# A two-layer attention and Fourier kernel: the transform along h taken apart into even and odd frequencies

## Chip, cores and metric

The kernel runs on one core of a Trainium2 chip. The metric is the device time of one execution in microseconds; the time before is a median of three runs. Arithmetic is in 32-bit floats throughout, except for two small bf16 mask tables.

## The reference

The input x is 8 images of 128 x 128 pixels with 64 channels (axes b, h, w, c). Two layers follow each other.

```
# layer 0: criss-cross attention, for every pixel along its column and its row
Q, K = x @ w_q, x @ w_k          # 8 channels each
V = x @ w_v                      # 64 channels
energy_H = Q . K along h, own pixel set to -inf
energy_W = Q . K along w
att = softmax over the 128 + 128 energies
x = gamma * (att_H V + att_W V) + x

# layer 1: a Fourier mixer, then a depthwise MLP
h  = layernorm(x) @ w_te                     # 128 channels
F  = fft2(h) over h and w
fc = gelu([re F, im F] @ w_fc)
x1 = x + real(ifft2(fc_re + i fc_im)) @ w_tp
h2 = layernorm(x1) @ w_fe                    # 128 channels
d  = gelu(3x3 depthwise convolution of h2)
out = x1 + d @ w_fp
```

The discrete transform is done with matrix products. A transform of 128 lines along h can be split: with s = line n + line n+64 and d = line n - line n+64, the even frequencies are a transform of the 64 lines of s, the odd ones of the 64 lines of d.

## The kernel before

The kernel has two stages that follow each other.

**attention()** goes over 64 tasks: for each image four H blocks and then four W blocks of 32 columns or lines. Step n of its loop turns and projects block n+1, computes the energies of n+1 and n in one pass, and finishes the products of n-1. The order of instructions on each engine is that of the loop's text. For W blocks a tail follows in later steps: `weigh` (n-1, ACT), `total` (n-1, POOL), `invert` (n-2, DVE), `combine` (n-2, POOL: the weighted sum of H and W parts onto x, and the store to x2), and the layer norm, `norm_step`, called four times in a step as parts 0 to 3. Parts 0 and 2 square half a block on ACT (L559) and sum x on DVE (L560), parts 1 and 3 sum the squares (L562), all for block n-4. Part 3 also takes the inverse root for block n-5 on POOL, and for every second W block packs two normed blocks, 64 lines, into the buffer `yw` (L574) and sends them to DRAM as one half of `xn` (L578). `yw` has two buffers, each holding the attention output of two W blocks and then the packed lines; the ACT copies of L409 fill it. In the first W pair of an image it is one buffer, in the second pair the other. For the last three blocks DVE does what POOL does else, and SP the stores.

**mixer()** does the rest. A planner, `Plan.run`, orders the work: every piece has an engine, a cost, a due time, what it follows, and the buffers ("slots") that it takes and frees. The planner is greedy: on each engine the ready piece with the earliest due time goes first. Due times come from the constants of the head (PERIOD, GROUP0, GROUP and so on), so the transforms of image b+1 and the MLP of image b are woven together. For one image the transforms are: `along_w` (PE, all 128 lines of 64 channels to 64 frequencies along w, real and imaginary), `along_h` on 17 groups of up to four frequencies, `keep_h` (ACT, PSUM to SBUF), `channels` (PE), `bend` (ACT, gelu), `hermite` (POOL), `project` (PE), `keep_g` (ACT), then `inverse_h`, `inverse_w` and `add` (DVE). The MLP: `turn`, `expand`, nine taps of the convolution (`first_tap` on ACT, most of the rest on DVE at L1144, some as ACT products that DMAs add, L1138), `bend`, `shrink`, `add` (L1211).

In the mixer PSUM has two slots "fc" of two banks and four slots "mm" of one bank. `along_w`, `along_h`, `project`, `inverse_h`, `inverse_w`, `turn`, `expand` (two at once) and `shrink` share the four. In `along_h` each frequency costs four products of 128 lines by 128 frequencies:

```
nc.tensor.matmul(fps[0:64, n, :], lhsT=re, rhs=cos, start=True, stop=False)
nc.tensor.matmul(fps[64:128, n, :], lhsT=im_, rhs=cos, start=True, stop=False)
nc.tensor.matmul(fps[0:64, n, :], lhsT=im_, rhs=sin, start=False, stop=True)
nc.tensor.matmul(fps[64:128, n, :], lhsT=re, rhs=nsin, start=False, stop=True)
```

A 32-bit product stands in the profile as two instructions.

Of the kernel before, what the change touches and what calls it, by code (L numbers as in the profile page):

```python
# [22 lines left out]
F32 = mybir.dt.float32  # L23
# [3 lines left out]
ALU = mybir.AluOpType  # L27
# [4 lines left out]
P = 128  # L32
C = 64
D8 = 8
HID = 128
R = 32
# [7 lines left out]
BY_DMA, BY_DMA_LAST = (1, 2), 1  # L44


PERIOD, GROUP0, GROUP, BACK0, BACK = 262.0, -1.9, 10.3, 174.8, 4.3
CHUNK0, CHUNK, STAY, LOADX = 18.2, 14.2, 0.1, -10.2
CH = 8
LN = 16  # L50

# [1 line left out]
def dft_tables():  # L53

    n = np.arange(P)
    kw = np.arange(64)
    ang = 2.0 * np.pi * (np.outer(n, kw) % P) / P
    rw = np.stack([np.cos(ang), -np.sin(ang)], axis=2)
    rw[:, 0, 1] = np.where(n % 2 == 0, 1.0, -1.0)
    rw = rw.reshape(P, P)  # L60
    full = 2.0 * np.pi * (np.outer(n, n) % P) / P
    cos, sin = np.cos(full), np.sin(full)
    k = np.arange(64)
    back = 2.0 * np.pi * (np.outer(k, n) % P) / P
    re = 2.0 * np.cos(back) / P
    re[0] = 1.0 / P
    im = -2.0 * np.sin(back) / P
    im[0] = np.where(n % 2 == 0, 1.0, -1.0) / P
    idw = np.concatenate([re, im], axis=0)
    out = np.concatenate([rw, cos, sin, -sin, cos / P, sin / P, -sin / P, idw], axis=1)  # L70
    return np.ascontiguousarray(out.astype(np.float32))


TBL_W = 8 * P


def border_marks():
# [164 lines left out]
def attention(tc, nc, x, w_q, b_q, w_k, b_k, w_v, b_v, gamma, x2, xn, prm, marks, packed):  # L242
    NB = x.shape[0]
    with ExitStack() as ctx:
# [202 lines left out]
        state = {}  # L447
# [27 lines left out]
        def maximum(n):  # L475

            b, way, blk = tasks[n]
            s, o = state[n], img[b]
            cols = slice(blk * R, blk * R + R)
            if way == "H":  # L480
                nc.vector.tensor_copy(o.mh[:, cols].rearrange("p (q i) -> p q i", q=4), s.mneg)
                return
            t = s.t = late.tile([P, 5, R], F32, tag="tsm", name="tsm", bufs=4)
            nc.gpsimd.tensor_tensor(
                t[:, 0, :].rearrange("p (q i) -> p q i", q=4),
                o.mdt[:, 0, cols].rearrange("p (q i) -> p q i", q=4), s.mneg, ALU.subtract,
            )
# [20 lines left out]
        def is_w(n):  # L508
            return 0 <= n < len(tasks) and tasks[n][1] == "W"
# [20 lines left out]
        def combine(n):  # L530
# [13 lines left out]
                    merger(n).tensor_tensor(xv, xv, part, ALU.add)  # L544
            store(n).dma_start(out=x2[b][:, blk * R : blk * R + R, :], in_=s.xb)

        def norm_step(n, part):


            m = n - 4  # L550
            if is_w(m):
                s = state[m]
                h = slice(16 * (part // 2), 16 * (part // 2) + 16)
                sq = s.y[:, h, 0:C]
                if part % 2 == 0:
                    if m >= N - 3:
                        nc.vector.tensor_tensor(sq, s.xb[:, h, :], s.xb[:, h, :], ALU.mult)
                    else:
                        nc.scalar.activation(sq, s.xb[:, h, :], AF.Square)  # L559
                    nc.vector.tensor_reduce(s.t[:, 0, h], s.xb[:, h, :], AX.X, ALU.add)  # L560
                else:
                    nc.vector.tensor_reduce(s.t[:, 1, h], sq, AX.X, ALU.add)  # L562
            m = n - 5
            if is_w(m):
                b, way, blk = tasks[m]
                s = state[m]
                r, q, t = (s.t[:, i, :] for i in range(3))
                if part == 3:
                    inverse_root(merger(m), m >= N - 3, r, q, t)
                if part == 3 and blk % 2 == 1:  # L570
                    z = s.yw.rearrange("p r c -> p (r c)")[:, 0 : 2 * R * C].rearrange("p (c r) -> p c r", c=C)
                    for o, lo in ((state[m - 1], 0), (s, R)):
                        for h in range(0, R, 8):
                            merger(m).tensor_tensor(  # L574
                                z[:, :, lo + h : lo + h + 8].rearrange("p c r -> p r c"), o.xb[:, h : h + 8, :],
                                o.t[:, 0, h : h + 8].unsqueeze(2).to_broadcast([P, 8, C]), ALU.mult,
                            )
                    (nc.sync if m >= N - 3 else nc.gpsimd).dma_start(out=xn[b][:, blk // 2, :, :], in_=z)  # L578

        def across(o, c0):  # L580

# [14 lines left out]
        N = len(tasks)  # L596
        E = mybir.EngineType
        with tc.manual_schedule(engines={E.PE, E.Activation, E.DVE, E.Pool}):
            for n in range(-1, N + 6):
# [18 lines left out]
                    moved(ps.tile([P, 2, 512], F32, tag="ps", name="mt"))  # L618
                if new is not None:
                    new.queries()  # L620
                norm_step(n, 0)
                if last is not None:
                    last.attend(1, 0, last.y)
                    across_all(n - 1)
# [2 lines left out]
                if new is not None:  # L627
                    new.values(0)
                flush(1)
                norm_step(n, 1)  # L630
                if is_w(n - 2):
                    invert(n - 2)
                if new is not None or old is not None:
                    for k in range(2):
                        energies(0, k, new, old, masked)
                norm_step(n, 2)
                if is_w(n - 1):
                    weigh(n - 1)
                if new is not None:
                    new.values(1)  # L640
                if old is not None:
                    target(n)
                    old.attend(0, 1, old.y)
                    old.attend(0, 0, old.y)
                flush(1)
                if new is not None or old is not None:
                    for k in range(2):
                        energies(1, k, new, old, masked)
                if is_w(n - 1):
                    total(n - 1)  # L650
                norm_step(n, 3)
# [8 lines left out]
def mixer(tc, nc, x2, xn, tbl, packed, spread, out):  # L660
    NB = out.shape[0]
    with ExitStack() as ctx:
# [6 lines left out]

        tb = const.tile([P, TBL_W], F32, tag="tb", name="tb")  # L670
        nc.sync.dma_start(out=tb, in_=tbl)
        rw, cos, sin, nsin, cosn, sinn, nsinn, idw = (tb[:, P * i : P * i + P] for i in range(8))
        pk = const.tile([P, PACKED], F32, tag="pk", name="pk")
        nc.sync.dma_start(out=pk, in_=packed[:, 0:PACKED])
        c = fields(pk, PARTS)
# [102 lines left out]
        class Image:  # L778
# [27 lines left out]
                    self.at = big([P, P, C], "at")  # L806
                nc.scalar.copy(self.at[:, :, c0 : c0 + 4], aps.rearrange("p c k -> p k c"))

            def along_h(self, g):

                at = self.at.rearrange("p (k t) c -> p k t c", t=2)
                fps = ps_m.tile([P, 4, P], F32, tag="mm", name="fps")
                for n, k in enumerate(g):
                    if k % 64 == 0:
                        a = at[:, 0, k // 64, :]
                        nc.tensor.matmul(fps[0:64, n, :], lhsT=a, rhs=cos, start=True, stop=True)
                        nc.tensor.matmul(fps[64:128, n, :], lhsT=a, rhs=nsin, start=True, stop=True)
                        continue
                    re, im_ = at[:, k, 0, :], at[:, k, 1, :]
                    nc.tensor.matmul(fps[0:64, n, :], lhsT=re, rhs=cos, start=True, stop=False)  # L820
                    nc.tensor.matmul(fps[64:128, n, :], lhsT=im_, rhs=cos, start=True, stop=False)
                    nc.tensor.matmul(fps[0:64, n, :], lhsT=im_, rhs=sin, start=False, stop=True)
                    nc.tensor.matmul(fps[64:128, n, :], lhsT=re, rhs=nsin, start=False, stop=True)
                return fps

            def keep_h(self, g, fps):
                f = pf.tile([P, 4, P], F32, tag="f", name="f", bufs=3)
                nc.scalar.copy(f[:, 0 : len(g), :], fps[:, 0 : len(g), :])  # L828
                return f

            def channels(self, g, f, half):
# [27 lines left out]
            def project(self, g, gr, gi):  # L859
# [3 lines left out]
                if g[0] == 0:  # L863

                    parts = (
                        (0, gr, 0, wtp, True, False), (0, gi, P, wtpn, False, False), (0, None, 0, btp, False, True),
                        (1, gi, 0, wtp, True, False), (1, gr, P, wtp, False, True),
                    )
                    for t, src, o, w, first, last in parts:
                        for z, zo in halves:  # L870
                            a = e0[:, z] if src is None else src[:, o + zo : o + zo + 64]
                            nc.tensor.matmul(gps[z, 0, t, :], lhsT=a, rhs=w, start=first, stop=last)
                    return gps
                for j in range(len(g)):
                    for t, src in enumerate((gr, gi)):
                        for z, zo in halves:
                            o = j * P + zo
                            nc.tensor.matmul(  # L878
                                gps[z, j, t, :], lhsT=src[:, o : o + 64], rhs=wtp, start=True, stop=True
                            )  # L880
# [65 lines left out]
        def transforms(b):  # L946
# [25 lines left out]
            for i, g in enumerate(GROUPS):  # L972
                n = len(g)
                t = t0 + GROUP0 + GROUP * i
                s, fs, hold = Slot("mm"), Slot("f"), {}
                p = plan.add(
                    "PE", 0.47 * n if i else 0.5, lambda g=g, hold=hold: hold.update(ps=im.along_h(g)), keeps, t, "C", (s,)
                )
                im.last_h.append(p)
                f = plan.add(  # L980
                    "ACT", 0.1 + 0.12 * n, lambda g=g, hold=hold: hold.update(f=im.keep_h(g, hold["ps"])), [p], t + 1,
                    takes=(fs,), frees=(s,),
                )
                sums, outs, p = [], [], None
                for half in range(2):
# [390 lines left out]
```

## Time and profile before

| what | value |
|---|---|
| median of three runs | 3202.73 us (3199.78 to 3213.37) |
| profiled execution | 3198.24 us |
| its span, first to last instruction | 3196.4 us |
| PE busy | 2915.1 us, 91% |
| DVE busy | 2486.9 us, 78% |
| ACT busy | 2096.0 us, 66% |
| POOL busy | 1636.0 us, 51% |
| L1144, taps on DVE | 840 of 1517 ns |
| L838, products of `channels` | 1088 of 598 ns |
| L828 and like copies of 128x512 on ACT | about 0.59 us each |
| L578, xn from POOL | 14 of 2048 KB, 9.4 us to landing |
| L545, x2 from POOL | 30 of 1024 KB, 4.9 us to landing |

Attention takes the first 1275 us or so, the mixer the rest. A row of the page gives line, engine, operation, tiles, shapes and count, then busy time and the mean of one in ns, then how long the engine had been idle before these instructions and which engine and line ended most of that wait. "issue" is a wait that the profile doesn't explain. Busy shares are means over stages with different limits.

### The profile page before, as it was taken

The numbers are of one execution on the slowest core, as the hardware profiler recorded it, in microseconds if no ns is written. First come the engines' busy times: TensorE is split into PE (matmuls) and PEld (weight loads), VectorE is DVE, ScalarE is ACT, GpSimd is POOL, SyncE is SP. The second block draws the span as 40 slices with busy tenths as digits, with TensorE's granted clock in tenths as the row PEclk, the third lists the DMA queues.
The fourth block names the chain that finished last, engine by engine and source line by source line (L and its number), as shares of the span: only waits on it lengthen the run. The fifth ranks groups of instructions, "written<-read, shape, count | busy, mean of one in ns | idle before, by whom it ended". The sixth has DMA issues, their size and how long they took to land.

```text
span 3196.4 us, 110388 instructions
## 1 busy us (share of the span) xinstructions
PE 2915.1 (91%) x50476; PEld 2144.6 (67%) x50476; DVE 2486.9 (78%) x2313; ACT 2096.0 (66%) x2744; POOL 1636.0 (51%) x1974
## 2 busy tenths in 40 slices
PE   7998898988888986999999999999999999999978
PEld 5877777777777776766666575675675675665644
DVE  4575747574747576819999999999999999999996
ACT  3665656565656654537868867767777777777754
POOL 1095959595959585424525516515525425435421
PEclk8999999999999998999999999999999999999989
DMA  6024242424243422242674664655745745745645
GB/s 175 23 96 121 96 130 99 121 95 121 101 132 104 122 95 104 99 159 50 134 172 89 157 144 85 170 117 93 182 105 108 176 96 111 178 94 100 120 90 100
DMA packets 227069, 372.71 MB, mean 117 GB/s; under 512 B 143401, under 2 KB 176812, under 8 KB 208044
## 3 DMA queue, kind: packets, MB, share of 16 engines
q0 software_dynamic: 37072, 188.39, 26.1%
q1 hardware_dynamic: 188764, 177.19, 19.7%
q8 instruction: 396, 6.49, 0.8%
q14 instruction: 69, 0.57, 0.1%
q10 hardware_dynamic: 768, 0.07, 0.0%
HBM read 170.96 MB, written 102.26 MB: 85 GB/s over the span
## 4 chain that ended last, share of the span: by engine, by line
PE 49%; DVE 29%; POOL 9%; issue 6%; DMA 4%; ACT 2%; SPq 0%; POOLq 0%; ACTq 0%; DVEq 0%
DVE acc L1144 16%; PE fcps L838 6%; PE yp L403 6%; PE e L433 4%; PE dps L906 4%; POOL xb L544 3%; PE yps L893 3%; PE yps L895 3%; DVE m L438 3%; PE vps L381 3%; PE tp L348 3%; DMA acc<-pr 3%; PE pq L362 3%; PE op L1206 3%; PE tpy L584 2%
## 5 line engine op out<-in xcount | busy, mean ns | idle before, releaser
L1144 DVE SCALAR_TENSOR_TENSOR acc<-h,pk,acc 128x1024 f32<-128x1024 f32 x840 | 1270.0, 1517 | 49.6 <-ACT acc L1130 28.1
L854 POOL TENSOR_TENSOR gs<-gl 128x512 f32<-128x512 f32 (+2 forms) x272 | 441.9, 1644 | 303.3 <-ACT gl L848 301.9
L838 PE MATMUL fcps<-f,pk 128*128 128x512 f32 (+2 forms) x1088 | 508.9, 598 | 0.2 <-ACT f L828 0.2
L438 DVE TENSOR_REDUCE m<-e 128x8 f32<-128x1024 f32 x256 | 300.6, 1211 | 211.5 <-PE e L433 211.3
L444 ACT ACTIVATE att<-e 128x1024 f32<-128x1024 f32 x256 | 259.7, 1024 | 170.2 <-PE e L433 166.3
L848 ACT ACTIVATE gl<-fcps,pk 128x1024 f32<-128x1024 f32 (+2 forms) x272 | 289.9, 1073 | 96.3 <-PE fcps L838 77.6
L1039 POOL TENSOR_TENSOR xc<-x,st 128x512 f32<-128x512 f32 x128 | 184.1, 1454 | 293.8 <-PE tpn L1073 117.1
L1138 POOL DMA_DIRECT2D acc<-pr x120 | 105.6, 880 | 443.4 <-DVE acc L1144 268.6
L403 PEld LDWEIGHTS yp<-v,att 128*64 128x64 f32 x8192 | 268.9, 143 | 87.3 <-issue 39.6
L433 PE MATMUL e<-kt,qt 32*128 32x128 f32 x4096 | 302.7, 291 | 25.4 <-DVE v L384 13.6
L838 PEld LDWEIGHTS fcps<-f,pk 128*128 128x128 f32 x1088 | 191.9, 193 | 196.2 <-issue 146.4
L403 PE MATMUL yp<-v,att 128*64 128x65 f32 x8192 | 296.8, 229 | 18.9 <-issue 17.3
L433 PE MATMUL e<-qt,kt 32*128 32x128 f32 x4096 | 300.1, 288 | 12.2 <-issue 10.1
L433 PEld LDWEIGHTS e<-kt,qt 32*128 32x128 f32 x4096 | 262.6, 194 | 38.1 <-DVE v L384 17.6
L433 PEld LDWEIGHTS e<-qt,kt 32*128 32x128 f32 x4096 | 258.6, 193 | 19.7 <-issue 13.1
L820 PE MATMUL fps<-tb,at 128*64 128x128 f32 x1008 | 200.4, 281 | 23.3 <-DVE ot L1211 23.3
L1134 ACT ACTIVATE pr<-h,pk 128x1024 f32<-128x1024 f32 x176 | 214.3, 1237 | 0.0
L878 PEld LDWEIGHTS gps<-pk,gs 128*64 128x64 f32 x4032 | 137.3, 144 | 108.7 <-issue 57.5
L1115 ACT ACTIVATE h<-hp,pk 128x512 f32<-128x512 f32 x254 | 156.4, 669 | 71.4 <-PE hp L1095 71.2
L384 DVE TENSOR_TENSOR v<-vps,bv 128x1024 f32<-128x1024 f32 x128 | 156.0, 1218 | 60.6 <-PE vps L381 60.6
L893 PE MATMUL yps<-tb,gt 128*64 128x128 f32 x1024 | 202.0, 279 | 0.6 <-ACT gt L887 0.6
L894 PE MATMUL yps<-tb,gt 128*64 128x128 f32 x1024 | 202.0, 279 | 0.0
(218 smaller groups left out, 7419.9 us busy)
## 6 DMA issues: line engine op xcount, KB each, us to landing
acc<-pr POOLq DMA_DIRECT2D x120, 512.0 KB, 5.4
xb<-in_x_dram SPq DMA_DIRECT2D x32, 1024.0 KB
xn<-xn SPq DMA_DIRECT2D x32, 1024.0 KB
x<-x SPq DMA_DIRECT2D x32, 1024.0 KB
x<-spread POOLq DMA_DIRECT2D x32, 1024.0 KB, 8.4
x<-xb POOLq DMA_DIRECT2D x30, 1024.0 KB, 4.9
out_dram<-ot SPq DMA_DIRECT2D x120, 256.0 KB
xn<-yw POOLq DMA_DIRECT2D x14, 2048.0 KB, 9.4
```

What stands on the lines that cost most here:

```text
L403: nc.tensor.matmul(yq[z, q, j, :], lhsT=att[:, q, j, z], rhs=self.v[:, r, :], start=True, stop=True)
L433: nc.tensor.matmul(e[:, q, j, :], lhsT=left[rows, 4 * a + j, :], rhs=right[rows, 4 * a + j, :], start=not msk, stop=j == 3 or not msk,)
L438: nc.vector.tensor_reduce(new.mneg[:, 2 * k : 2 * k + 2, 4 * a : 4 * a + 4], e1, AX.X, ALU.max, negate=True,)
L444: nc.scalar.activation(att, e2, AF.Exp)
L820: nc.tensor.matmul(fps[0:64, n, :], lhsT=re, rhs=cos, start=True, stop=False)
L838: nc.tensor.matmul(ps[:, sgn, 0:n], lhsT=w[:, cols], rhs=fv, start=True, stop=not mean)
L848: nc.scalar.activation(gl[:, :, 0:n], ps[:, :, 0:n], AF.Gelu, bias=bfc[:, half : half + 1])
L854: nc.gpsimd.tensor_tensor(gs[:, 0:n], gl[:, 0, 0:n], gl[:, 1, 0:n], ALU.add if half == 0 else ALU.subtract)
L893: nc.tensor.matmul(yps[0:64, c, :], lhsT=gr, rhs=cosn, start=True, stop=False)
L894: nc.tensor.matmul(yps[64:128, c, :], lhsT=gi, rhs=cosn, start=True, stop=False)
L1134: nc.scalar.activation(pr, self.lines(k, t), AF.Identity, bias=zero, scale=wdw[:, t : t + 1])
L1144: nc.vector.scalar_tensor_tensor(out=a, in0=self.lines(k, t), scalar=wdw[:, t : t + 1], in1=a, op0=ALU.mult, op1=ALU.add)
```

## The change

Attention no longer stores the first and the last 64 normed lines of an image, but their sum (slot 0 of `xn`) and their difference (slot 1). The first pair of blocks is written to both slots by one DMA with a broadcast source. The second pair is then added to slot 0 by two accumulating DMAs of half the channels each, and subtracted from slot 1: one step later ACT makes negated copies `zn` of 16 channels, and four accumulating DMAs add them. For the last image DVE makes sum and difference, and SP stores both. Parts 0, 1 and 2 of `norm_step` move to later places of the step, and the copy of an H block's maximum moves from DVE to ACT.

In the mixer `along_w` gets sums in its first 64 rows and differences in the last 64. `along_h` treats two groups in one piece of work: each frequency takes eight products of 64 rows by 64 frequencies, on the four quadrants of the array, into two PSUM banks (even and odd). `keep_h` copies from both banks, and the banks come free after the second group's copy. The frequency order within a group is now even, then odd; the inverse's tables are permuted to it. The planner's constants and two of its costs change.

```diff
-PERIOD, GROUP0, GROUP, BACK0, BACK = 262.0, -1.9, 10.3, 174.8, 4.3
-CHUNK0, CHUNK, STAY, LOADX = 18.2, 14.2, 0.1, -10.2
+PERIOD, GROUP0, GROUP, BACK0, BACK = 261.3, -4.6, 10.2, 174.7, 4.5
+CHUNK0, CHUNK, STAY, LOADX = 16.0, 14.9, 0.4, -18.3
+ZN = 3
+AH = 0.33
...
             if way == "H":
-                nc.vector.tensor_copy(o.mh[:, cols].rearrange("p (q i) -> p q i", q=4), s.mneg)
+                nc.scalar.copy(o.mh[:, cols].rearrange("p (q i) -> p q i", q=4), s.mneg)
...
+        def packed_lines(n):
+            return state[n].yw.rearrange("p r c -> p (r c)")[:, 0 : 2 * R * C].rearrange("p (c r) -> p c r", c=C)
...
-                    (nc.sync if m >= N - 3 else nc.gpsimd).dma_start(out=xn[b][:, blk // 2, :, :], in_=z)
+                    if m < N - 3 and blk == 1:
+                        nc.gpsimd.dma_start(out=xn[b], in_=z.unsqueeze(1).to_broadcast([P, 2, C, 2 * R]))
+                    elif m < N - 3:
+                        for c in (slice(0, 32), slice(32, C)):
+                            nc.gpsimd.dma_start(out=xn[b][:, 0, c, :], in_=z[:, c, :], accum_op=ALU.add)
+                    elif blk == 3:
+                        z0 = packed_lines(m - 2)
+                        nc.vector.tensor_tensor(z0, z0, z, ALU.subtract)
+                        nc.vector.scalar_tensor_tensor(out=z, in0=z, scalar=2.0, in1=z0, op0=ALU.mult, op1=ALU.add)
+                        nc.sync.dma_start(out=xn[b][:, 0, :, :], in_=z)
+                        nc.sync.dma_start(out=xn[b][:, 1, :, :], in_=z0)
+            m = n - 6
+            if is_w(m) and tasks[m][2] == 3 and m < N - 3 and part:
+                for c in ((0,), (1,), (2, 3))[part - 1]:
+                    c = slice(16 * c, 16 * c + 16)
+                    zn = late.tile([P, 16, 2 * R], F32, tag="zn", name="zn", bufs=ZN)
+                    nc.scalar.mul(zn, packed_lines(m)[:, c, :], -1.0)
+                    nc.gpsimd.dma_start(out=xn[tasks[m][0]][:, 1, c, :], in_=zn, accum_op=ALU.add)
...
                     new.queries()
-                norm_step(n, 0)
...
                 flush(1)
-                norm_step(n, 1)
...
                         energies(0, k, new, old, masked)
-                norm_step(n, 2)
+                norm_step(n, 0)
...
                     new.values(1)
+                norm_step(n, 1)
...
                         energies(1, k, new, old, masked)
+                norm_step(n, 2)
...
-            def along_h(self, g):
+            def along_h(self, gs):
...
-                fps = ps_m.tile([P, 4, P], F32, tag="mm", name="fps")
+                fps = [ps_m.tile([P, 8, 64], F32, tag="mm", name="fps") for _ in range(2)]
+                rows = (slice(0, 64), slice(64, 128))
...
+                    for t, (w, v) in enumerate(((cos, cos), (sin, nsin))):
+                        for ps, r in zip(fps, rows):
+                            nc.tensor.matmul(
+                                ps[0:64, n, :], lhsT=at[r, k, t, :], rhs=w[r, :], start=t == 0, stop=t == 1
+                            )
+                            nc.tensor.matmul(
+                                ps[64:128, n, :], lhsT=at[r, k, 1 - t, :], rhs=v[r, :], start=t == 0, stop=t == 1
+                            )
...
-                nc.scalar.copy(f[:, 0 : len(g), :], fps[:, 0 : len(g), :])
+                fv = f.rearrange("p k h -> p (k h)")[:, 0 : n * P].rearrange("p (z k h) -> p z k h", z=2, k=n)
+                for z in range(2):
+                    nc.scalar.copy(fv[:, z, :, :], fps[z][:, lo : lo + n, :])
...
-                p = plan.add(
-                    "PE", 0.47 * n if i else 0.5, lambda g=g, hold=hold: hold.update(ps=im.along_h(g)), keeps, t, "C", (s,)
-                )
+                if i % 2 or i == 0:
...
+                    gs, pair, banks = (GROUPS[i : i + 2] if i else GROUPS[0:1]), {}, (Slot("mm"), Slot("mm"))
+                    along = plan.add(
+                        "PE", AH * sum(map(len, gs)) if i else 0.5, lambda gs=gs, pair=pair: pair.update(ps=im.along_h(gs)),
+                        keeps, t, "C", banks,
+                    )
+                    im.last_h.append(along)
+                second = i > 0 and i % 2 == 0
                 f = plan.add(
-                    "ACT", 0.1 + 0.12 * n, lambda g=g, hold=hold: hold.update(f=im.keep_h(g, hold["ps"])), [p], t + 1,
-                    takes=(fs,), frees=(s,),
+                    "ACT", 0.3 + 0.12 * n, lambda g=g, hold=hold, pair=pair, lo=4 * second: hold.update(
+                        f=im.keep_h(g, pair["ps"], lo)), [along], t + 1,
+                    takes=(fs,), frees=banks if second or i == 0 else (),
                 )
```

## The prediction

> **What bounds the kernel now.** I read the page's slices first, then busy time by stretch, the chain of waits, and the timeline around the places where the chain changes engine.
>
> ```profile
> PE   7998898988888986999999999999999999999978
> DVE  4575747574747576819999999999999999999996
> POOL 1095959595959585424525516515525425435421
> ```
>
> A slice is 80 us. Up to slice 16 (attention, to about 1275 us) no engine is full, and POOL swings between 9 and 5. From slice 18 on (the mixer) PE and DVE are both at 9.
>
> *Attention.* The seven first-pair DMAs of L578 are issued at 260.9, 414.8, 570.4, 724.6, 879.9, 1034.9 and 1187.4 us, so an image takes about 154 us. Why 154? The POOL and ACT timelines:
>
> ```profile
> 314.31 0.25 POOL L522 TENSOR_TENSOR tsm<-mdt,tsm 128x32 f32<-128x32 f32 x1 [12.19 <-ACT tsm L516]
> ```
>
> ```profile
> 398.43 1.18 POOL L544 TENSOR_TENSOR xb<-xb,yw 128x512 f32<-128x512 f32 x1
> 399.90 0.63 POOL L545 DMA_DIRECT2D x<-xb  x1 [0.30 <-POOL xb L544]
> ...
> 406.41 8.11 POOL L574 TENSOR_TENSOR yw<-xb,tsm 128x512 f32<-128x512 f32 x8
> 414.82 0.62 POOL L578 DMA_DIRECT2D xn<-yw  x1 [0.30 <-POOL yw L574]
> ```
>
> ```profile
> 424.37 1.09 ACT L409 COPY yw<-yp 128x520 f32<-128x520 f32 x2 [4.56 <-POOL tsm L104]
> 734.21 1.09 ACT L409 COPY yw<-yp 128x520 f32<-128x520 f32 x2 [3.68 <-DMA xn<-yw]
> ```
>
> POOL starts at 314.31, when ACT's weights arrive, and has no gap worth naming until it issues the first pair's xn DMA at 414.82: 100.5 us. That DMA lands after 9.4 us (the page's median), at 424.2. Only then is the buffer yw free, and ACT, idle for 4.56 us, writes the next image's first W block into it. The row names POOL, whose roots happened to end there; two images later it names the DMA. From ACT's restart (270.49 in the image before) to POOL's next start are 43.8 us. So the period is **a ring**: 43.8 (PE and ACT) + 100.5 (POOL) + 9.5 (DMA) = 153.8. Anything added to these three lengthens attention; what lies beside POOL's 100 us is free.
>
> In that transfer the DMA engines are full (fields: stretch, length, busy time and count of PE, PEld, DVE, ACT, POOL, then clock, DMA share, GB/s):
>
> ```profile
> 414.80:424.30 9.50, 8.97 (x238) 7.96 (x228) 4.81 (x4) 3.13 (x3) 7.55 (x29) 1.00 1.05 334
> ```
>
> 334 GB/s over 9.5 us is 3.2 MB: the 2.1 of xn and the 1.05 of one block's load.
>
> *Mixer.* One image's period, from one along_w to the next, and what DVE waits for over five such periods (1667 to 2817 us):
>
> ```profile
> 1896.00:2126.70 230.70, 217.48 (x2624) 147.48 (x2622) 214.11 (x190) 173.02 (x230) 101.29 (x80) 0.97 0.59 129
> ```
>
> ```profile
> DVE ot L1211 <- PE op L1206: 39.5, 35, 4.9
> DVE x L914 <- PE dps L906: 13.6, 23, 0.9
> ```
>
> DVE works 214 of 230 us and waits for PE 53.1/5 = 10.6. That is all a faster PE can return in a period. Image 0 differs: 1293 to 1444 us has no MLP beside it and is PE's chain throughout.
>
> **What the Trainium skill says.** (1) "TensorE: Matmul & The Clock Gate", Part 3 (row/col tiling): matmuls on different row and column groups of the array run concurrently. The trace agrees: values() puts 64 instructions on four 64x64 quadrants in 1.09 to 1.16 us, while the old along_h, on two column halves, takes 3.49 us for 64 (tile fps):
>
> ```profile
> 414.00 1.16 PE L381 MATMUL vps<-wv,xt 64*64 64x64 f32 x64
> ```
>
> ```profile
> 1347.88:1351.37 3.49, 3.49 (x64) 3.42 (x64) 0.58 (x1) 1.00 0.30 127
> ```
>
> (2) "TensorEngine Tiling (Array Packing)", Gotcha 1: row tiles write to different PSUM banks. The new along_h takes two banks at once; no run shows what that costs yet. (3) "DMA: Bandwidth & Descriptors", Issuing engines are not separate DMA queues: all DMAs share 16 engines. The share of 1.05 above agrees. (4) The same page, Rules for kernel authors: an accumulating DMA must wait for an earlier DMA on the same bytes; relevant below.
>
> **The change, part by part.**
>
> *Transform along h, PE.* Eight frequencies were 64 instructions, 3.49 us. They become 128 of half the length. At values()'s 17 ns each (1.09/64): 2.18 us. Saved 1.31 per eight, times 63/8: **10.3 us an image**. Bounds: nothing gained beyond the plan's own figure of 0.33 a frequency (0.436-0.33, 6.7 us), or the full 10.3; I take 10.
>
> *keep_h, ACT.* One copy of 128x512 (0.59, L828) becomes two of 128x256 (0.41, L1108): +0.23 x 16 = 3.7 us an image. ACT works 173 of 230, which hides it; without that cover it is 3.7.
>
> *Two banks held.* Four "mm" slots serve along_w, project, turn, expand and the inverse; a pair now holds two until the second keep_h. Behind a waiting along_h stands all of PE. Bounds 0 to 5 us an image; with the new order constants, whose effect no row shows, I take it as the reason why only part of the gain is returned.
>
> *What the mixer returns.* Image 0: all 10. Images 1 to 7: between 0 and 10; PE-bound stretches alternate with DVE-bound ones and DMA chains (pr into pr, pr into acc), so I take 4.5. Sum 10 + 31.5 = **-42 us**.
>
> *First pair's DMA, POOL to DRAM.* It now writes both slots: 4 MB instead of 2, and yw is released when it has landed. The extra 2.1 MB cost 5.0 us at the best rate seen (421 GB/s), 6.3 at 334, 9.4 at its own present pace. I take 6.5, with its dearer issue. ACT's stall of 4 to 6 us becomes 11 to 12, and behind it stand PE's next energies. It is in the ring: 7 x 6.5 = 45.5, less 2, since two of the seven stalls (580.7, 1045.0) ended about 1 us after the landing. (The last image goes another way.)
>
> *Second pair.* Two accumulating DMAs of 1 MB, then four negating ACT copies (about 1.05 us each, from L559's square of the same shape) with four accumulating DMAs of 512 KB. Issues: POOL goes from 2 x 0.62 to about 0.8 + 6 x 0.88 (L1138's accumulate) = 6.1, +4.9 us. They fall where POOL waits 10.9 and 12.2 us for ACT's weights; without that cover, 5 us an image. Their slot was written by the first pair's DMA, landed by then (issued at 414.8, needed at 435.8). The buffer they read is next written at 470.7; x<-spread's 8.4 us per accumulated MB frees it near 453. But three of the copies stand before the next block's xt copies on ACT, in the 43.8 us of the ring: +3. And PE's issue gaps (1.5 us at 426, 2.1 at 447) sit around these transfers, which get longer: +1. Bounds 0 to 9, I take 4: **28 us**.
>
> *Norm's parts moved, H's maximum on ACT.* One W block's four parts (two squares of 1.06 us on ACT, four sums of 1.21 on DVE) move behind energies and values of the same step, and 32 copies of 0.62 us leave DVE for ACT (estimate 0.25 each, from L514's 0.22 of that shape). All of it is in H steps, beside POOL's 100 us; POOL's roots, which need the sums, come some 15 us or more later. Nothing, either way. Without that cover, 2 us an image.
>
> *Last image.* Two DVE operations of 128x4096, about 4.8 us each (four times L557's 1.2), once, and SP stores both halves at the end. The mixer's DVE first works after a wait of 54.7 us, which covers it; uncovered, 10 us in all.
>
> **Sum**: +43.5 + 28 - 42 = about +30 on the profiled execution's 3198.2, so 3228. The median of the runs shown is 4.5 above that execution: **3233 us**.
>
> **Rivals.**
>
> *PE is what the mixer lacks* (ends faster). All of DVE's wait for PE goes: 10 + 7 x 10 = -80. With attention at its low end (7 x 5 + 7 x 1 = +42) that is -38: 3165. It decides from where the mixer's return exceeds attention's loss by 16 us. For: PE at 94% and DVE's 10.6 us. Against: at my attention figure of 71.5 even the full return gives only 3194.
>
> *Accumulation chokes the DMA engines.* Broadcast at 9.4, ring part at 9, two banks eating the gain outside image 0: 7 x 18.4 - 10 = +119: 3322. For: engines at 1.05 already. Against: nothing in attention but the yw stall waits long for a transfer.
>
> *The quadrants don't overlap*, so the change doesn't do what it says: 55 ns an instruction (3.49/64) for twice as many is +27 us an image, +220 with attention's 71 on top: about 3490. values()'s row speaks against it.
>
> **How the numbers follow.** The forecast 0.60 (its own range 3208 to 3275), PE's gain 0.21, choked DMA 0.16, no overlap 0.03. About 0.5%, 16 us, is what a measurement of this kernel tells from no change. Faster: 0.20 of PE's gain. Same: the forecast's lower end, 0.14, and 0.01. Slower: 0.65. The range 3170 to 3305 leaves out the lower part of PE's gain (0.08), the upper of choked DMA (0.09) and the last.
>
> **What would show it.** Right: L409's wait for yw at 10 us or more in every image; the first-pair issues some 164 us apart; 4096 KB landing in about 16 us; eight frequencies of fps in about 2.2 us; mixer periods near 225. Wrong: an attention period at or below 156, or mixer periods at 219 with DVE no longer waiting for op.

## The result, and the profile after

The changed kernel takes **3296.68 us** (median of four runs, 3290.59 to 3302.06); the kernel before, run beside it on the same chip, 3204.58. The ratio is 1.029, interval 1.0266 to 1.0314: about 92 us slower. The forecast was 3233. Its profiled execution has a span of 3288.8 us against 3196.4.

The slices of the page, in the same units as before (here 82 us each):

```profile
PE   7997979898988986499899888898898898898878
DVE  4574747474746566706998999999989999989996
POOL 1095959595958685232433523624515425425321
```

Attention (up to slice 16) has the same swing on POOL. At slice 16 (counted from 0), where attention hands over to the mixer, PE falls to 4, where before had a 9. DVE's dip one slice later was there before (0 now, 1 then). In the mixer PE has 8s where it had 9s, and DVE is at 9 as before.

I divide the loss by the start of each image's along_w in the two traces:

| stretch | before, us | after, us | loss |
|---|---|---|---|
| start to image 0's along_w | 1275.5 | 1308.8 | +33.3 |
| image 0 to image 1 | 168.7 | 206.1 | +37.4 |
| image 1 to image 7, six periods | 6 x 228.8 | 6 x 232.0 | +19.3 |
| image 7 to the end | 379.6 | 382.0 | +2.4 |

The third row is not even: 8.9 us of it lie in the first of the six periods (222.9 before, 231.8 after), and 2.1 us in each of the others.

**Attention.** The first-pair DMAs are now issued at 258.8, 419.0, 576.9, 735.6, 896.0, 1054.9 and 1212.9 us, 159.0 apart (154.4 before). The source view of the new DMA line, L591, gives its duration and who waited for it:

```profile
L591 POOL DMA_DIRECT2D xn<-yw x7: 719/719/732, 258.8 to 1212.9; - x7
...
  ACT yw L416: 92.5, 7
...
DMA to landing us min/median/max: 14.1/14.6/15.0
```

The same view of before's L578:

```profile
L578 POOL DMA_DIRECT2D xn<-yw x14: 622/624/630, 260.9 to 1209.0; - x14
...
  ACT yw L409: 10.3, 2
...
DMA to landing us min/median/max: 7.9/9.4/9.6
```

ACT's copy into yw now waits for this transfer in all seven images, 13.2 us each. ACT's timeline shows one of them, and the windows view of after shows that the DMA engines are full meanwhile (fields as in the prediction):

```profile
433.61 1.09 ACT L416 COPY yw<-yp 128x520 f32<-128x520 f32 x2 [14.15 <-DMA xn<-yw]
```

```profile
419.00:433.70 14.70, 4.23 (x116) 3.78 (x108) 1.71 (x2) 0.55 (x2) 12.05 (x41) 0.78 1.04 369
```

**Handover.** POOL's waits between 1300 and 1480 us have a row that before's don't have, and POOL's timeline shows where it ends:

```profile
POOL gs L894 <- DVE yw L586: 53.6, 1, 53.6
POOL gs L894 <- ACT gl L888: 50.5, 29, 6.7
```

```profile
1368.26 10.99 POOL L894 TENSOR_TENSOR gs<-gl 128x256 f32<-128x256 f32 x3 [53.55 <-DVE yw L586]
```

The first gs, the output tile of `hermite` in the mixer, waits for attention's packing of the last image's lines into yw (L586, on DVE). These two have nothing to do with each other in the computation. Behind gs stands project, and with it PE. The windows view for 20 us of that wait:

```profile
1350.00:1370.00 20.00, 0.00 (x0) 0.00 (x0) 19.21 (x43) 0.00 (x0) 1.74 (x1) 0.50 0.00 0
```

PE and ACT do nothing at all while DVE finishes attention's last norms.

**Mixer.** One period, and DVE's waits over five periods (1746.7 to 2906.8 us):

```profile
1981.70:2211.60 229.90, 205.77 (x3133) 136.67 (x3132) 216.61 (x190) 174.26 (x247) 96.12 (x80) 0.96 0.59 128
```

```profile
DVE ot L1257 <- PE op L1252: 32.9, 26, 3.0
DVE x L954 <- PE dps L946: 18.5, 22, 2.1
```

In this period PE works 205.8 us, and in the mean of the five 207.3, against 217.2 before: it has lost the 10 us that it was to lose. DVE still waits 10.3 us a period for it (before: 10.6), and the period has not become shorter. PE's own waits over the same five periods tell where its time went. After:

```profile
PE tpn L1119 <- DVE ot L1257: 34.2, 5, 7.5
PE op L1252 <- ACT acc L1237: 25.5, 17, 3.2
PE gps L918 <- POOL gs L894: 25.4, 18, 3.0
```

and before:

```profile
PE fps L820 <- DVE ot L1211: 19.4, 5, 3.9
PE gps L878 <- POOL gs L854: 15.7, 10, 3.4
PE gps L878 <- DVE ot L1211: 14.8, 7, 2.9
```

PE gets to `turn` (tpn), `shrink` (op) and `project` (gps) earlier and waits there for DVE, ACT and POOL: these three rows are 85.1 us after, the three largest of before 49.9, in five periods. PE's saving became PE's waiting.

### The profile page after: what moved, and what is told of

It is laid out like the page before. It is cut to its first block, busy times and chain, and to the rows that moved or that the text cites. A ratio compares the mean times of both kernels' runs of the same rounds, so it can differ in the third digit from the quotient of the medians.

```text
span 3288.8 us, 118951 instructions
## 1 busy us (share of the span) xinstructions
PE 2848.8 (87%) x54572; PEld 2058.7 (63%) x54572; DVE 2499.2 (76%) x2283; ACT 2132.9 (65%) x2940; POOL 1627.3 (49%) x2009
## 5 line engine op out<-in xcount | busy, mean ns | idle before, releaser
L1190 DVE SCALAR_TENSOR_TENSOR acc<-h,pk,acc 128x1024 f32<-128x1024 f32 x840 | 1290.3, 1539 | 42.9 <-ACT acc L1176 22.1
L894 POOL TENSOR_TENSOR gs<-gl 128x512 f32<-128x512 f32 (+2 forms) x272 | 423.5, 1580 | 328.7 <-ACT gl L888 260.5
L410 PEld LDWEIGHTS yp<-v,att 128*64 128x64 f32 x8192 | 258.0, 137 | 95.6 <-PE pq L369 38.5
L410 PE MATMUL yp<-v,att 128*64 128x65 f32 x8192 | 287.4, 224 | 25.8 <-issue 18.4
L1085 POOL TENSOR_TENSOR xc<-x,st 128x512 f32<-128x512 f32 x128 | 171.0, 1359 | 182.0 <-PE tpn L1119 100.0
L1252 PEld LDWEIGHTS op<-pk,acc 128*64 128x64 f32 x4096 | 139.9, 145 | 115.1 <-ACT acc L1237 83.3
L954 DVE TENSOR_TENSOR x<-dps,x 128x512 f32<-128x512 f32 x128 | 87.9, 686 | 151.7 <-PE dps L946 150.9
## 6 DMA issues: line engine op xcount, KB each, us to landing
xn<-yw POOLq DMA_DIRECT2D x7, 4096.0 KB, 14.6
```

The lines of the kernel that those rows point to most:

```text
L410: nc.tensor.matmul(yq[z, q, j, :], lhsT=att[:, q, j, z], rhs=self.v[:, r, :], start=True, stop=True)
L894: nc.gpsimd.tensor_tensor(gs[:, 0:n], gl[:, 0, 0:n], gl[:, 1, 0:n], ALU.add if half == 0 else ALU.subtract)
L1085: nc.gpsimd.tensor_tensor(xc, self.x[:, rows, :], self.st[:, 0, rows].unsqueeze(2).to_broadcast([P, CH, C]), ALU.mult)
L1190: nc.vector.scalar_tensor_tensor(out=a, in0=self.lines(k, t), scalar=wdw[:, t : t + 1], in1=a, op0=ALU.mult, op1=ALU.add)
```

## The experiments

All ratios are against the kernel before on the same chip (3198 to 3201 us). "Image 0" is the time from its along_w to image 1's; "period" is the mean of the six that follow, if nothing else is said. How far such numbers scatter is seen where the code is the same: in the five traces with before's attention (before, e3, e6, e11, e14) the first along_w starts at 1269.0 to 1280.7 us and attention's period is 154.1 to 155.5; before and e2, with the same mixer, have periods of 228.8 and 229.0; the four changed mixers of after, e1, e3 and e4 have 231.8 to 232.6.

**First batch: where the loss sits.** Theory: attention's ring pays for the broadcast transfer, and zn's place in SBUF makes the handover wait. Rivals: the accumulating DMAs or the negated copies cost attention, and the mixer's new form costs the handover.

*e1*: zn in a pool of its own, opened last, so that no other tile's address moves.

```diff
+        zpool = ctx.enter_context(tc.tile_pool(name="a_zn", bufs=ZN))
...
-                    zn = late.tile([P, 16, 2 * R], F32, tag="zn", name="zn", bufs=ZN)
+                    zn = zpool.tile([P, 16, 2 * R], F32, tag="zn", name="zn", bufs=ZN)
```

> The changed kernel, with the negated copies zn in a pool of their own behind all others of attention, so that every other tile of attention lies where it lay in the kernel before. Theory 1 (addresses: the 12 KB of zn push attention's last packed lines under the mixer's first gs tiles, whose first write then waits for the last image's stores): POOL's wait of 53.6 us before its first gs goes, image 0's transforms take 159 to 169 us instead of 206, and the time falls by 37 to 47 us to about 3250 to 3260. Rival (the last image's longer tail on DVE delays the mixer whatever the addresses): 206 us and 3297 stay.

Measured: 3261.53 us, ratio 1.0193 (1.0174 to 1.0213). Image 0 171.5 us instead of 206.1, attention and periods unchanged (159.5, 232.4). In e1's windows view the same 20 us look like this:

```profile
1350.00:1370.00 20.00, 19.69 (x417) 12.67 (x414) 19.69 (x25) 11.69 (x17) 12.55 (x8) 1.00 0.01 2
```

The 35 us were a matter of addresses: e1 changes nothing but where zn lies. With zn's three tiles (12 KB a partition) in the pool `late`, the mixer's gs waited for yw; that it had come to lie on bytes which attention still used is inferred from this wait and from its going.

*e2*: e1's attention with before's mixer, whose 128-row tables are block-diagonal here so that it can take sums and differences. *e3*: before's attention with the changed mixer, which gets the plain lines; its transform is therefore not the reference's.

```diff
 e2, against the changed kernel:
-        cos, sin, nsin = (tb[:, 5 * P + 64 * i : 5 * P + 64 * i + 64] for i in range(3))
+        cos[64 * z : 64 * z + 64, 64 * z : 64 * z + 64] = np.cos(half)
...
-                        for ps, r in zip(fps, rows):
+                    nc.tensor.matmul(fps[0:64, n, :], lhsT=re, rhs=cos, start=True, stop=False)
 e3: attention() is that of the kernel before
```

> The attention of the changed kernel (zn in its own last pool) with the mixer of the kernel before: along_h keeps its four 128-row products a frequency and takes block-diagonal tables, planner constants as before. Attention alone costs the ring's 5 us an image, first along_w at about 1309 instead of 1275; mixer periods stay at 230 and image 0 at 169: 3205 + 33 = 3238. If the sums and accumulating DMAs also hurt the mixer, its periods are over 231 here; if the new along_h and its order are what lengthens them, they are at 229 to 231.

> The attention of the kernel before with the mixer of the changed kernel (the transform gets plain lines instead of sums and differences; only its time is of use). Theory (DVE is the floor of a mixer period, so PE's 10 us come back only in image 0): first along_w at 1275, image 0 159, periods 232 as in the changed kernel: 3205 - 10 + 20 = about 3210 to 3220. Rival (PE's relief does shorten the periods and the rest of the changed kernel hides it): periods 225, about 3165.

Measured: e2 3241.42 us, 1.0126 (1.0099 to 1.0153): attention +33.0, image 0 177.7 (169 was expected), period 229.0. e3 3218.33 us, 1.0057 (1.0039 to 1.0075): image 0 161.7, period 232.6. So attention's half costs 43 us and the mixer's half 20, together the 63 that e1 costs. The rest of the 92 us is zn's place: 29 by the medians, each against its own control, and 34.6 in image 0 of the two traces. The changed mixer alone loses: it gains 7 us in image 0, where PE is the chain, and loses 3.8 in each period.

*e4*: e1, but the first pair goes to slot 0 only, and SP copies slot 0 to slot 1 in DRAM a step later.

```diff
-                        nc.gpsimd.dma_start(out=xn[b], in_=z.unsqueeze(1).to_broadcast([P, 2, C, 2 * R]))
+                        nc.gpsimd.dma_start(out=xn[b][:, 0, :, :], in_=z)
...
+            if is_w(m) and tasks[m][2] == 1 and m < N - 3 and part == 3:
+                nc.sync.dma_start(out=xn[tasks[m][0]][:, 1, :, :], in_=xn[tasks[m][0]][:, 0, :, :])
```

> As e1, but POOL stores the first pair to slot 0 only (2 MB), and SP copies slot 0 to slot 1 inside DRAM one step later, which holds no buffer of attention. Theory 2 (ring of 43 + 101 + the first pair's landing): landing back at about 9.4 us, attention's period from 158.9 to about 153.7, 36 us less than e1: about 3215 to 3225. Rival (the accumulating DMAs or the moved norm parts make the period): it stays at 158 or more, time as e1.

Measured: 3229.76 us, 1.0093 (1.0067 to 1.0119). Attention's period is 155.2 us, along_w starts at 1283.2. In the source view of its DMA line:

```profile
  ACT yw L417: 23.8, 3
...
DMA to landing us min/median/max: 8.8/9.6/9.7
```

The landing falls from 14.6 to 9.6 us and the period by 4.3 (159.5 in e1); ACT's wait for it is found in three images instead of seven, 7.9 us each. The negated copies and all accumulating DMAs are still there: together they cost some 0.8 us an image (155.2 - 154.4), no more than the scatter of this number. The ring is confirmed, and the rival of dear accumulation falls. A 2 MB copy within DRAM, on another queue, beside the work, costs next to nothing where the same bytes in the ring cost 4.3 us an image.

**Second batch: the mixer's period**, with e4 as the base. Candidates: DVE's work, the planner's constants, two banks held by a pair.

*e6* and *e8*: one more tap of each second chunk goes from DVE to ACT products and DMAs, in the kernel before (e6) and in e4 (e8).

```diff
-BY_DMA, BY_DMA_LAST = (1, 2), 1
+BY_DMA, BY_DMA_LAST = (2, 2), 1
```

> The kernel before with BY_DMA (2, 2): the control to e8. If PE with 217 us of 229 is the next bound there, the period falls by 3 us at most: about 3180 to 3200. If it falls by 10 us as well, PE's relief is of no use at all to the mixer and DVE was the only floor: about 3130.

> e4 with BY_DMA (2, 2) instead of (1, 2): in every second line block one more tap leaves DVE and becomes an ACT product that a DMA adds, 8 taps of 1.64 us less on DVE an image, 8 products of 1.24 us more on ACT. Theory 3 (DVE's work is the floor of a mixer period now that PE has 10 us less): period from 232 to about 222, 3230 - 7 x 10 = about 3160, faster than the kernel before. Rival (DVE's own work isn't it; the chains of product, DMA, gelu and shrink in front of op are): period 230 or more, 3220 or more.

Measured: e6 3527.67 us, 1.1021 (1.0984 to 1.1058), period about 280 (last five). e8 3471.01 us, 1.0843 (1.0807 to 1.0879), period about 268. DVE's work fell to 190 and 193 us a period, and its wait for op rose to 68 and 61. The added products and DMAs seem to set the time here: in e6 PE waits 34 us a period for ACT's acc before op. e6 lies outside both of its expectations. e8 lies on the rival's side, but its edit lengthens the very chain that the rival names. So neither says whether DVE was a limit before.

*e7*: e4 with before's planner constants. *e9*: e4 with along_h on one group at a time, its two banks freed by its own keep_h.

```diff
 e7:
-PERIOD, GROUP0, GROUP, BACK0, BACK = 261.3, -4.6, 10.2, 174.7, 4.5
-CHUNK0, CHUNK, STAY, LOADX = 16.0, 14.9, 0.4, -18.3
+PERIOD, GROUP0, GROUP, BACK0, BACK = 262.0, -1.9, 10.3, 174.8, 4.3
+CHUNK0, CHUNK, STAY, LOADX = 18.2, 14.2, 0.1, -10.2
 e9:
-                    gs, pair, banks = (GROUPS[i : i + 2] if i else GROUPS[0:1]), {}, (Slot("mm"), Slot("mm"))
+                    gs, pair, banks = [g], {}, (Slot("mm"), Slot("mm"))
...
-                    takes=(fs,), frees=banks if second or i == 0 else (),
+                    takes=(fs,), frees=banks,
```

> e4 with the planner constants of the kernel before (PERIOD to LOADX; along_h's own cost of 0.33 stays). If the new constants are what makes the periods 232 instead of 229, they come back to 229: 3230 - 20 = about 3210. If the new along_h does (two banks held, more copies), they stay at 232 or grow.

> e4 with along_h done for one group at a time: the same products, the two banks free again after that group's own keep_h instead of the second group's. If the held banks cost, the periods fall from 232 towards 229 or below: 3205 to 3215. If not, 232 and 3230 stay, or it gets longer by more switches on PE.

Measured: e7 3235.83 us, 1.0116 (1.0093 to 1.0139), period 232.2. e9 3285.62 us, 1.0272 (1.0249 to 1.0296), period 240.2. The constants are not the cause. e7 answers one more rival: in the changed mixers DVE's taps are slower (217.8 us of DVE's work a period after, 213.6 before), but in e7 DVE works 213.8, and the period (231.9 in the last five) is as long. Freeing the banks earlier doesn't help: going through single groups costs 8 us a period more, with 6 us more of PE's work. It does not clear the two banks, though, since here each single group takes both.

**Third batch: is it PE or DVE?**

*e11*: the kernel before without the sine half of along_h's products; planner, order and buffers as they were.

```diff
-                    nc.tensor.matmul(fps[0:64, n, :], lhsT=re, rhs=cos, start=True, stop=False)
-                    nc.tensor.matmul(fps[64:128, n, :], lhsT=im_, rhs=cos, start=True, stop=False)
-                    nc.tensor.matmul(fps[0:64, n, :], lhsT=im_, rhs=sin, start=False, stop=True)
-                    nc.tensor.matmul(fps[64:128, n, :], lhsT=re, rhs=nsin, start=False, stop=True)
+                    nc.tensor.matmul(fps[0:64, n, :], lhsT=re, rhs=cos, start=True, stop=True)
+                    nc.tensor.matmul(fps[64:128, n, :], lhsT=im_, rhs=cos, start=True, stop=True)
```

> The kernel before, with the sine half of along_h's products left out (two instead of four a frequency, so its output isn't the transform) and the planner's costs, hence every order, as before: PE alone gets 14.6 us less an image, nothing else changes. If a mixer period is DVE's and PE's relief is worth nothing in it, periods stay at 227 to 229 and only image 0 gains: 3198 - 14 to - 25. If DVE's 10.6 us of waiting for PE are PE's load, as the prediction had it, periods fall by 5 to 10: 3110 to 3150.

Measured: 3185.28 us, 0.9955 (0.994 to 0.997). Image 0 falls from 168.7 to 156.1. The periods stay: 228.2 against 228.8. The windows view and DVE's waits over five of them:

```profile
1658.40:2802.70 1144.30, 1029.28 (x11846) 671.63 (x11843) 1066.48 (x946) 862.10 (x1150) 505.71 (x400) 0.96 0.59 130
```

```profile
DVE ot L1209 <- PE op L1204: 40.7, 32, 4.7
DVE x L912 <- PE dps L904: 11.1, 20, 0.9
```

PE works 205.9 us a period instead of 217.2, and DVE waits 51.8/5 = 10.4 us for it, as before (10.6). This settles the step that I got wrong: DVE's wait for PE is not for PE's load. With the order fixed, DVE waits some 8 us a period for op whether PE is at 94% or at 90%.

*e10* and *e12*: e4 with hermite's subtraction (e10), or sum and subtraction (e12), taken from POOL and done by a second accumulating product in project. Buffers gl and gs change from 2 and 3 to 3 and 2, and the planner's order changes with the new pieces.

```diff
+                    if i and half in FOLD:
+                        sums.append(a)
+                        outs.append(gl)
+                        continue
...
-                    "PE", 0.23 * n if i else 0.9, ...
+                    "PE", 0.23 * n * (1 + 0.5 * len(FOLD)) if i else 0.9, ...
```

> e4, with POOL's subtraction of the two gelu halves (every second gs, 16 an image) replaced by two accumulating products in project, with weights wtp and wtpn: PE +8.5 us an image (from 206 to 215), POOL -26 us. Theory (DVE's 214 to 218 us hold some 35 us in which taps wait for POOL's gs and xc[...]: taps take 1.28 us alone, 1.63 on average): taps get faster by 0.1 us, DVE falls to about 205 and the period from 232 to 222 to 226: 3230 - 40 to - 70, which is faster than the kernel before. Rival (taps are slowed by something else): taps stay at 1.63 and the period at 232 or, with PE's load, more.

> e10 with both halves folded (all groups but the first): PE +17 us (to 224), POOL -52 us, taps down by 0.2 us to 1.43. DVE would fall to 195, so PE is the bound: period 228 to 233, about 3210 to 3240. If it is at 225 or below, PE's load counts less than its busy time says.

Measured: e10 3276.42 us, 1.0233 (1.0202 to 1.0263); e12 3306.70, 1.0341 (1.0301 to 1.0382). Image 0 is 225.4 and 233.5 us: the changed buffers moved addresses again, it seems, and now ACT's copy into f waits for attention's last transfer. ACT's, POOL's and PE's waits of e10 from 1270 to 1500 us have:

```profile
ACT f L873 <- DMA xn<-yw: 58.6, 1, 58.6
PE fcps L883 <- ACT f L873: 56.8, 1, 56.8
```

In the periods of e10 DVE's work fell from 216.5 to 199.8 us, as fewer POOL operations lie beside its taps, and the period did not fall (232.5, e4 231.8; e12 233.9). Here the order changed too, so this did not yet clear DVE.

**Fourth batch: less DVE work with the order fixed.** The ninth tap is done on one of its eight lines only; seven eighths of it are left out. *e14* does so to the kernel before, *e13* to e4.

```diff
-                a = self.out_lines(k)
+                a, h = self.out_lines(k), self.lines(k, t)
+                if t == 8:
+                    a, h = a[:, 0:1, :], h[:, 0:1, :]
```

> The kernel before, with the ninth tap of the convolution done on one of its eight lines only (seven eighths of that tap is left out); planner, orders and buffers unchanged. DVE loses 16 x 1.28 = about 20 us of its 214 a period, PE keeps its 217. If DVE's work, with PE's answers as fixed delays between, sets the period: it falls from 229 towards PE's 217 to 220, the total by 7 x 9 to 7 x 12 = 63 to 84 us, to about 3125. If chains across engines in the fixed orders set it: within 3 us of 229 a period, DVE's waits grow by what its work loses, total 3175 to 3200.

> e4 with the same cut: the ninth tap on one of eight lines only (seven eighths of it left out). PE has 207 us a period here, DVE 216 before the cut and about 196 after. If DVE sets the period, it falls from 232 to about 212, lower than the kernel before with the same cut, since PE's floor is lower by 10: the total falls by 7 x 20 = 140, to about 3090. If chains in the fixed orders set it: about 229 to 232, total 3210 to 3230.

Measured: e14 3142.94 us, 0.9822 (0.9793 to 0.9851); e13 3165.51 us, 0.9898 (0.9865 to 0.9932). Five periods of each in the windows view, the kernel before first, then e14, then e13:

```profile
1667.10:2816.80 1149.70, 1086.06 (x13104) 734.46 (x13102) 1067.91 (x946) 865.69 (x1150) 508.87 (x400) 0.97 0.59 129
```

```profile
1665.00:2776.10 1111.10, 1068.19 (x13104) 720.92 (x13102) 977.03 (x946) 865.47 (x1150) 512.03 (x400) 0.99 0.61 134
```

```profile
1688.50:2802.60 1114.10, 1026.09 (x15663) 679.98 (x15662) 997.51 (x946) 870.75 (x1235) 495.00 (x400) 0.97 0.61 134
```

DVE lost 18.2 us a period in e14 and the period 7.7: some 40% comes back. In e13 it lost 17.0 and the period 8.7, half of it. So DVE's work counts in part, where PE's counted for next to nothing. And both end at 222 to 223 us in these five periods, although PE works 213.6 in one and 205.2 in the other: with a lighter DVE too, PE's saving does not show. This last is no clean test, since the two differ in their orders as well and DVE works 4 us more in e13 (199.5 against 195.4). The waits of DVE for op in e14 rise to twice those of before:

```profile
DVE ot L1213 <- PE op L1208: 79.1, 51, 3.3
```

Neither theory held whole. No engine's load sets the period by itself. What is left are chains that pass from engine to engine in the fixed orders, in which DVE's work is one part; this is argued from what the runs exclude, and no run shows such a chain. Which it is, and why the changed mixer's periods are 3 us longer (3.8 in e3), stays open. e7 rules out the constants. The two banks that a pair takes, the order as a whole, and PE's clock, which was granted at 0.95 to 0.96 in the changed mixers' last five periods and at 0.97 before, were not tested apart.

No kernel here beats the kernel before with the whole computation done. Splitting along h in image 0 alone was not tried; e3 puts it at 7 us before what attention pays.

## Why the prediction was wrong

The sign was right, the size was not: +30 forecast, +92 measured. The terms, with what the traces give for each:

| term | forecast, us | measured, us |
|---|---|---|
| first pair's DMA | +43.5 | +28.4 (start of along_w, e1 less e4) |
| second pair | +28 | +4.9 (the rest of attention's 33.3) |
| image 0's transform | -10 | -7.0 (e3) |
| images 1 to 7 | -31.5 | +21.7 (19.3 and 2.4) |
| last image | 0 | +9.0 (e2) |
| addresses | not in the sum | +34.6 (after less e1) |

These are single traces, so each can be off by some us. The right sign is in part luck: attention at its measured 33 with the forecast's return of 42 would have made the kernel faster by 9.

- **First pair's DMA: right as mechanism, too large.** The ring of POOL, DMA and ACT was the mechanism. The extra landing was 5.2 us (14.6 - 9.4) where I took 6.5: 369 GB/s, between the two rates that I had as bounds. POOL's 100.5 are 101.0, PE and ACT's 43.8 are 43.3, and 43.3 + 101.0 + 14.7 gives the 159.0 measured.
- **Second pair, +28: wrong.** It measured some 0.8 us an image (e4), about 5 in all. The copies do stand ahead of the next block's xt copies on ACT:

```profile
461.98 2.94 ACT L606 ACTIVATE zn<-yw 128x1024 f32<-128x1024 f32 x3
```

 but the way from ACT's restart to POOL's next start is 43.3 us with them, 43.8 without. I had added their length to a stretch without showing that ACT, and not PE, is what that stretch waits for.
- **Transform on PE: right as work, wrong as time.** Eight frequencies take 2.35 us in the trace (forecast 2.18, before 3.49), in the windows view with the tile fps alone:

```profile
1425.00:1440.00 15.00, 2.35 (x128) 2.08 (x128) 2.35 (x8) 1.00 0.01 2
```

 The quadrants overlap: an instruction of half the length takes 18 ns here, where the old one took 55. PE's work fell by 9.9 us a period. The step that failed is what I made of DVE's wait for PE. I called its 10.6 us "all a faster PE can return in a period", which no run contradicts as a bound, and took 4.5 of it as coming back in each of seven images, -31.5. Next to nothing came back: with 11.3 us less of PE's work and the order fixed, e11's period is 0.6 us shorter and DVE's wait is 10.4. The changed periods even are 3 us longer, for a reason that stays open. DVE's wait for an answer of PE was read as a lack of PE's time.
- **Image 0, -10: right alone, lost in the whole.** e11 gained 12.6 and e3 7.0 there, where PE is the chain. In the changed kernel image 0 lost 37.4: 35 by the addresses, 9 by the last image (next point), less the 7. (e11's 12.6 is no measure of the split: it leaves out half of the products.)
- **Costed at nothing, and not: the last image.** The two DVE operations of 128x4096 were put behind DVE's own wait of 54.7 us. What they hold up is POOL. In e1, DVE's and then POOL's timeline:

```profile
1384.70 4.42 DVE L598 TENSOR_TENSOR yw<-yw 128x4096 f32<-128x4096 f32 x1
1389.16 5.37 DVE L599 SCALAR_TENSOR_TENSOR yw<-yw 128x4096 f32<-128x4096 f32 x1
```

```profile
1386.26 3.98 POOL L895 TENSOR_TENSOR gs<-gl 128x512 f32<-128x512 f32 x1 [4.29 <-ACT gl L889]
1390.21 5.44 POOL L895 TENSOR_TENSOR gs<-gl 128x512 f32<-128x512 f32 x1
```

 Two gs take 3.98 and 5.44 us beside them; the next, alone, takes 1.27. PE's project then waits 5.07 us for gs. The Trainium skill states the cause in "SBUF — State Buffer", SBUF: two separate sides: a DVE operation with two SBUF inputs and a GpSimd operation that reads SBUF exclude each other at a shared port, for the whole instruction. These durations agree: each of the two gs ends 1.1 us after the DVE operation beside it (1389.12 and 1394.53), as if it had begun when that one was done. e2, whose mixer is that of before, has image 0 at 177.7 against 168.7: 9 us, near the 10 that I had named for the case without cover. PE's waits for gs in image 0, before and in e2, make 5.8 of them:

```profile
PE gps L878 <- POOL gs L854: 1.0, 1, 1.0
PE gps L908 <- POOL gs L884: 6.8, 3, 5.1
```

 The other 3.2 are PE's own work (169.6 us against 166.5, at a granted clock of 0.96 against 0.98), for which no run shows a reason. So the sum came near 10 by a way that I had not named: the cover was looked for on the wrong engine.
- **Not in the sum at all: SBUF addresses.** The new tile zn, 12 KB a partition, went through the prediction as a copy and a DMA, never as memory that shifts what the next stage lies on. It is the largest single loss, 35 us.
- **The rivals.** "PE is what the mixer lacks" fell with e11. "Accumulation chokes the DMA engines" was nearest in time (3322) and wrong in its reason: with the accumulating DMAs still there, e4's first pair lands after 9.6 us, as before.

## What to carry to other kernels

A wait of one engine for another is not a measure of what a faster other engine returns: cut the other's work with the order fixed (as e11 did) before counting on it. A tile added in one stage is also a change of addresses in the next; look at the first instructions after the handover for a wait on a tile of the old stage, and open the new pool last. Put bytes that no one waits for onto another queue: 4.3 us an image went away by copying in DRAM instead of holding a buffer for a transfer of twice the bytes.

## What I had not expected of the hardware

- Accumulating DMAs to DRAM were cheap for POOL, which issues them: 0.86 us for 512 KB and 1.05 for 1 MB (a plain store of 2 MB: 0.62). They land after about 6 us for 512 KB and, two in a row, 9 to 18 us for 1 MB each (median 12.5), with no one on the path waiting.
- POOL's operations weigh on DVE's taps, which fits the shared port above. Over five periods of the kernel before, 264 taps without a POOL tensor operation beside them take 1281 ns in the mean, 256 with one take 1958. DVE's "busy" 214 us a period holds this waiting, some 35 us by these means (256 x 0.68 / 5, an estimate). With half of POOL's gs gone (e10) the mean tap fell from e4's 1631 to 1473 ns.
- While 2 MB of SBUF were stored to two places, 4 MB, the DMAs reached 369 GB/s over 14.7 us with all engines full, more than the 334 over the 2 MB store's 9.5. Both figures hold a block's load beside the store.
